# A transformer layer with butterfly networks on one core: loads in a fixed order, one order of work for each sequence, W_up transposed in two halves, the second folded matrix built on GpSimd

## The chip, the core and the metric

The kernel runs on one core of a Trainium2 chip. The metric is the device time of one execution in microseconds. Before the change the median of three runs is 900.11 us (900.03 to 900.91). Engines are called by the profile's names: PE (matrix products), PEld (its weight loads), DVE (VectorE), ACT (ScalarE), POOL (GpSimd), SP (the queue from which most DMAs are issued).

## The reference

Eight sequences of 512 rows and 256 columns go through a feed-forward block, attention and the same feed-forward block again, all in float32:

```python
def ffn(x):                                   # used twice, with the same weights
    h = x @ W_exp + b_exp                     # 256 -> 1024
    h = butterfly(h, up_weights, 1024)        # 10 stages of 2x2 mixes, stride 2**stage
    h = gelu(h + up_bias)
    h = butterfly(h, down_weights, 1024)
    return h @ W_con + b_con + down_bias      # 1024 -> 256

x = x + 0.5 * ffn(layernorm(x))
x = x + attention(layernorm(x))               # 16 heads of 32 (two halves of 16), causal softmax, then @ Wo
x = x + 0.5 * ffn(layernorm(x))
```

A butterfly is linear, so W_exp with the first network is one 256x1024 matrix W_up, and the second network with W_con one 1024x256 matrix W_dn.

## The kernel before

**The start (lines 613 to 632)** builds W_up and W_dn once on the chip. `low_matrices` (L201) multiplies the seven low stages of a network into one 128x128 matrix for each of 8 blocks of rows: six elementwise products at L223 with 32, 64, ..., 1024 elements per partition, on DVE. `low_up` (L244) multiplies the blocks of W_exp by them on PE. `high_stage` (L227) does one of the three high stages: for each of 8 blocks ACT or POOL scales the block itself (L236, L238, into `mine`), and DVE adds the scaled partner block (L241). `finish_up` (L261) transposes the result on PE with 16 transposes (L267) and copies it to `wup_sb` in four copies, two on ACT and two on DVE (L268). Then come the up products of sequence 0 (`up_steps`, L307 on PE, the Gelu at L314 on ACT), three between the stages of the second network; the second network's matrices (DVE, ahead of them), its three high stages, and `low_down` (L270), whose products (L273) make W_dn. `keep_busy(26)` (L255) runs 26 filler products at the very start. Row norms are `ln_stats` (L148: DVE, and POOL for the power at L158) and `ln_apply` (L165); `ffn_bias` (L186) adds half of the two output biases to x on POOL (L189). The order of instructions in this part is that of the program, engine by engine.

**The loads (lines 117 to 135)** are issued from SP and ACT ahead of that part, without `manual_schedule`, so that the framework orders them.

**The main part (lines 634 to 636)** walks through 8 sequences. For each, `sequence` (L573) reads a string of tokens from `ORDER` and issues the work of each token, which fixes the order of every engine's queue. A token is a letter and a number; a digit ahead repeats it, and "+1" or "-1" behind it means that the work belongs to the next or the last sequence. On an entry "None" falls whatever sequence has no string of its own (1 to 4 here).

- f, F: one up product (128 hidden columns: L307, Gelu L314) and half a down product (L325; the sum into x at L334) of the first block; g, G the same of the second block, whose result is stored (L336). F and G fill one PSUM bank with two row tiles, t = 0 and 1, then 2 and 3.
- q, v, w: products for query or key (L350), value (L368), and output (L505).
- u: the scores of one of ten units (L404), then on DVE the mask and the row's minimum (L418), then the exponential on ACT (L431). The scores have one buffer of four banks (`ps_u`).
- t: DVE's transpose of exponentials within 32x32 blocks (L449, L453); m: the sums (L458, L459) and 16 DMAs that move the blocks to other partitions (L471, tile `pt`, one buffer); p: probabilities times values (L484), scaled into `ot` (L491).
- s, a, x with a, 1 or 2 behind: row norm's statistics, its application, and its transposition, which for most sequences is a DMA to memory (L287) and four back (L294). l: load a sequence's x (four buffers).

Products of q, v, f, F, g, G and w all take one of three PSUM buffers (`ps_a`).

Of the kernel before, what the change touches and what calls it, by code (L numbers as in the profile page):

```python
# [36 lines left out]
F32 = mybir.dt.float32  # L37
# [11 lines left out]
def macaron_kernel(  # L49
# [55 lines left out]
    def load_x(b):  # L105
        xt[b] = resid.tile([P, NT, C], F32, name=f"x_{b}", tag="x", bufs=4)
        nc.sync.dma_start(out=xt[b], in_=x[b].rearrange("(t p) c -> p t c", p=P))
# [7 lines left out]
    wdn_sb = const.tile([P, NBLK, C], F32, name="wdn_sb")  # L115

    last = upe_sb.shape[1] - NBLK * P
    nc.sync.dma_start(out=upe_sb[:, :last], in_=up_e[:, :last])
    nc.sync.dma_start(out=upe_sb[:, last:], in_=up_e[:, last:])
    for blocks in (slice(0, NBLK // 2), slice(NBLK // 2, NBLK)):  # L120
        nc.sync.dma_start(out=wexp_sb[:, blocks, :], in_=wexp_t.rearrange("(n p) c -> p n c", p=P)[:, blocks, :])
        if blocks.start == 0:
            load_x(0)
    nc.scalar.dma_start(out=upc_sb, in_=up_c)
    nc.scalar.dma_start(out=bc_sb, in_=b_con.to_broadcast([P, C]))
    nc.scalar.dma_start(out=db_sb, in_=dn_b.to_broadcast([P, C]))
    nc.scalar.dma_start(out=upb_sb, in_=up_b)
    nc.scalar.dma_start(out=dnc_sb, in_=dn_c)
    nc.sync.dma_start(out=dne_sb, in_=dn_e)
    nc.sync.dma_start(out=wcon_sb, in_=wcon.rearrange("(n p) c -> p n c", p=P))  # L130
    load_x(1)
    for w_sb, w in ((wq_sb, wq), (wk_sb, wk), (wv_sb, wv), (wo_sb, wo)):
        nc.sync.dma_start(out=w_sb, in_=w.rearrange("(k p) f -> p k f", p=P))
    for b in range(2, 4):
        load_x(b)


    ident = const.tile([P, P], F32, name="ident")
# [59 lines left out]
    kept = {}  # L198


    def low_matrices(tables, net):  # L201

        at, mat = 0, None
        for step in range(LOW):
            half = 1 << step
            mine = tables[:, at : at + NBLK * 2 * half].rearrange("p (n e) -> p n e", n=NBLK)  # L210
            at += NBLK * 2 * half
            if mat is None:
                mat = mine
                continue
            new = fold_pool.tile([P, NBLK, 2 * half], F32, name=f"mat_{net}_{step}", tag=f"mat_{step % 2}")
            if net == "up":
                dims, old = "p n (a r) -> p n a r", mat.rearrange("p n (o r) -> p n o r", o=1)
                shape = dict(a=2)
            else:
                dims, old = "p n (m b) -> p n m b", mat.rearrange("p n (m o) -> p n m o", o=1)  # L220
                shape = dict(b=2)
            view = new.rearrange(dims, **shape)
            nc.vector.tensor_tensor(view, mine.rearrange(dims, **shape), old.to_broadcast(view.shape), ALU.mult)  # L223
            mat = new
        return mat

# [31 lines left out]
        for _ in range(times):  # L258
            nc.tensor.matmul(idle[:, :P], lhsT=ident, rhs=ident, start=True, stop=True)  # L259

    def finish_up(cur, whole):  # L261
        nc.gpsimd.tensor_tensor(bup_sb, whole[:, :, C], upb_sb, ALU.add)
        for q in range(NBLK // 4):
            for kc in range(KC):
                pt = ps_a.tile([P, 512], F32, name=f"pup_{kc}_{q}", tag="a")
                for i in range(4):
                    nc.tensor.transpose(pt[:, bass.ts(i, P)], cur[4 * q + i][:, bass.ts(kc, P)], ident)  # L267
                (nc.vector.tensor_copy if kc else nc.scalar.copy)(wup_sb[:, kc, bass.ts(q, 512)], pt)  # L268

    def low_down(mats, cur):  # L270
        for blk in range(NBLK):
# [46 lines left out]
    def down_steps(b, what, store):  # L318
        def step(t, half):
            t2, i = divmod(t, 2)  # L320
            if i == 0 and half == 0:
                kept["py", what, b] = ps_a.tile([P, 512], F32, name=f"py_{what}_{b}_{t2}", tag="a")
            g, py = kept["g", what, b], kept["py", what, b].rearrange("p (t c) -> p t c", c=C)
            for fc in range(half * NBLK // 2, (half + 1) * NBLK // 2):
                nc.tensor.matmul(  # L325
                    py[:, i, :],
                    lhsT=g[:, fc, bass.ts(t, P)],
                    rhs=wdn_sb[:, fc, :],
                    start=(fc == 0),
                    stop=(fc == NBLK - 1),  # L330
                )
            if i == 1 and half == 1:
                mine = xt[b][:, 2 * t2 : 2 * t2 + 2, :]
                nc.vector.scalar_tensor_tensor(mine, py, 0.5, mine, ALU.mult, ALU.add)  # L334
                if store:
                    nc.sync.dma_start(  # L336
                        out=out[b, bass.ds(2 * t2 * P, 2 * P), :].rearrange("(t p) c -> p t c", p=P), in_=mine
                    )

        return [partial(step, t, half) for t in range(NT) for half in range(2)]  # L340
# [177 lines left out]
    def run(*steps):  # L518
        for step in steps:
            if isinstance(step, list):  # L520
                run(*step)
            else:
                step()

    def attention_steps(b, pool):
        def moved(g):
# [15 lines left out]


    ORDER = {
        0: """3F+0 x1+1 F+0 2s1+2 sa+0 F+0 x1+1 3F+0 sa+0 2aa+0 2f+1 2xa+0 a1+2 f+1 q+0 a1+2 q+0 f+1 u0 q+0 v u1
              2q+0 t0 x1+2 t1b q+0 u2 t1a v t2a f+1 m0 2f+1 u3 f+1 v t2b u4 F+1 t3 F+1 v x1+2 u5 t4a 2F+1 t4b sa+1
              p0 m1 2F+1 aa+1 t5 2F+1 q+0 sa+1 u6 aa+1 q+0 t6b xa+1 u7 xa+1 t6a t7a p1 m2 u8 2q+1 u9 t8 t7b t9b
              2q+1 t9a 3q+1 p2 q+1 m3""",
        None: """u0 5f+1 u1 f+1 t1a 2f+1 u2 t0 p-3 v u3 t2a 3w-1 t1b m0 s2-1 w-1 v s2-1 u4 v 2F+1 a2-1 s1+2 a2-1 F+1
              t3 F+1 t2b x2-1 s1+2 F+1 v u5 t4a p0 t4b 2F+1 x2-1 m1 F+1 g-1 sa+1 4g-1 aa+1 2g-1 t5 sa+1 aa+1 g-1  # L550
              u6 2G-1 u7 p1 G-1 xa+1 t6a xa+1 q+1 t7a t6b m2 G-1 q+1 u8 t7b a1+2 t8 a1+2 q+1 x1+2 G-1 q+1 G-1 u9
              2G-1 x1+2 t9a t9b q+1 p2 q+1 l+3 m3 2q+1""",
        5: """u0 3f+1 s1+2 u1 f+1 s1+2 f+1 u2 t0 f+1 p-3 t1a t1b u3 2w-1 t2a s2-1 2w-1 m0 2f+1 u4 v s2-1 2a2-1 v
              t2b F+1 t4a t3 3F+1 u5 x2-1 a1+2 2v F+1 x2-1 t4b a1+2 u6 x1+2 p0 F+1 m1 F+1 u7 F+1 sa+1 2g-1 sa+1
              aa+1 2g-1 t7a aa+1 g-1 xa+1 t5 t6a 2g-1 xa+1 u8 t6b p1 m2 g-1 G-1 u9 2G-1 q+1 t8 t9b G-1 t7b q+1
              x1+2 q+1 2G-1 t9a p2 m3""",
        6: """u0 q+0 G-2 u1 G-2 f+1 t1b t1a q+0 u2 f+1 t0 q+0 f+1 t2b u3 t2a p-3 m0 q+0 u4 v l+2 t3 w-1 f+1 u5 w-1
              t4b t4a w-1 s2-1 w-1 2v a2-1 v u6 p0 m1 f+1 q+0 3f+1 t6b t6a t5 s2-1 u7 a2-1 3F+1 x2-1 u8 x2-1 F+1
              t7a p1 m2 u9 sa+1 3F+1 t9b F+1 2g-1 sa+1 2aa+1 t9a g-1 xa+1 g-1 t8 g-1 t7b g-1 p2 g-1 xa+1 g-1 m3
              3q+1""",  # L560
        7: """u0 q+0 u1 G-2 t0 G-2 u2 p-3 w-1 v t1a G-2 t1b t2a m0 u3 G-2 t2b w-1 u4 s2-1 v t4a w-1 t3 w-1 2v s2-1
              t4b p0 m1 2a2-1 2q+0 u5 q+0 u6 q+0 x2-1 G-2 t5 t6b u7 t6a G-2 x2-1 t7a p1 m2 G-2 t7b u8 G-2 2g-1 t8
              g-1 u9 t9b g-1 t9a 2g-1 p2 g-1 m3 g-1 7G-1 p3 2w+0 s2+0 2w+0 s2+0 a2+0 G-1 a2+0 2x2+0 8g+0 8G+0""",
    }
    LNS = {"a": "at", "1": "f1", "2": "f2"}
    queues = {}
# [4 lines left out]
        return queues[key, b].pop(0)  # L571

    def sequence(b, pool):  # L573
        for token in ORDER.get(b, ORDER[None]).split():
            times, rest = (int(token[0]), token[1:]) if token[0].isdigit() else (1, token)
            what, kind, at = rest[0], "", 0
            if what in "sax":
# [33 lines left out]


    with fold, tc.manual_schedule():
        keep_busy(26)
        mats = low_matrices(upe_sb, "up")
        nc.vector.tensor_tensor(bhalf, bc_sb, db_sb, ALU.add)
        nc.vector.tensor_scalar(bhalf, bhalf, 0.5, None, ALU.mult)
        cur = low_up(mats)
        run([partial(ln_stats, 0, "f1", half) for half in range(2)])
        run([partial(ln_apply, 0, "f1", half, nc.gpsimd) for half in range(2)])  # L620
        for i in range(HIGH):
            cur, whole = high_stage(cur, i, upc_sb, "up", C + 1, NBLK)
        run(ln_steps(0, "f1", copy=nc.scalar.copy), partial(ffn_bias, 0, 0), partial(ffn_bias, 0, 1))
        finish_up(cur, whole)
        up = up_steps(0, "f1")
        mats = low_matrices(dne_sb, "dn")
        cur = [wcon_sb[:, blk, :] for blk in range(NBLK)]
        for i in range(HIGH - 1, -1, -1):
            cur, _ = high_stage(cur, i, dnc_sb, "dn", C, NBLK if i == HIGH - 1 else NBLK // 2)
            run([up.pop(0) for _ in range(min(3, len(up)))])  # L630
        low_down(mats, cur)
        run(lns(1, "f1"))

    with tc.tile_pool(name="attn", bufs=1) as attn, tc.manual_schedule():
# [79 lines left out]
```

## Time and profile before

| | us |
|---|---|
| median of three runs | 900.11 |
| the profiled execution | 900.17 |
| its span, first to last instruction | 898.5 |
| PE busy | 871.0 |
| DVE busy | 628.8 |
| ACT busy | 516.0 |
| POOL busy | 87.1 |
| DMA engines, share of the span (queue 1) | 54.9% |

The mean granted clock of PE is 0.989. "Busy" of PE includes the filler products (8.8 us). The span is what the trace covers; the execution's own time is 1.67 us longer. A group's line has the engine, the operation, output and input, the count, then busy time and mean length; the costliest are L325 (233.9 us in 1024 instructions), L307 (229.7 in 512) on PE, and L431 (280.3) and L418 (216.2) on ACT and DVE. A stretch's line has, for each engine, busy time and the number of instructions, in the order PE, PEld, DVE, ACT, POOL, then the granted clock of PE, the share of the DMA engines and GB/s.

### The profile page before, as it was taken

What the parts mean: (1) busy time and instruction counts of PE and PEld (TensorE: products, weight loads), DVE (VectorE), ACT (ScalarE), POOL (GpSimd) and SP (SyncE); (2) the same over time, 40 slices, a digit from 0 to 9 for tenths busy, and PEclk for the clock granted to TensorE, in tenths of its full rate; (3) what the DMA queues carried; (4) which work ended last, traced back from release to release, by engine and by line L of the source; (5) the groups of instructions that cost most, each with busy time, mean ns of one, the idle gap of its engine ahead of it and who ended that gap; (6) DMA issues with size and microseconds to landing.
All of it is one profiled execution on the core that took longest, in us unless ns stands there. A gap on an engine that the chain in (4) does not pass through costs nothing.

```text
span 898.5 us, 13295 instructions
## 1 busy us (share of the span) xinstructions
PE 871.0 (97%) x4348; PEld 502.6 (56%) x4348; DVE 628.8 (70%) x1812; ACT 516.0 (57%) x1356; POOL 87.1 (10%) x103
## 2 busy tenths in 40 slices
PE   6999979999999999999999999999999999999998
PEld 5574633565645655465554656456564573644656
DVE  6966885685838867397675968589868875888230
ACT  4718746944558364763648445695749764756211
POOL 4230000020100201020010201002000010010010
PEclk8899989999999999999999999999999999999999
DMA  9110667366571657546392665816775577477600
GB/s 327 61 47 24 159 186 174 70 177 175 151 201 44 173 136 210 142 117 171 107 249 62 173 170 128 234 53 171 184 191 131 142 199 195 103 177 192 151 12 23
DMA packets 52931, 130.15 MB, mean 145 GB/s; under 512 B 10880, under 2 KB 32640, under 8 KB 52864
## 3 DMA queue, kind: packets, MB, share of 16 engines
q1 hardware_dynamic: 52144, 129.00, 54.9%
q8 instruction: 34, 0.56, 0.3%
q10 hardware_dynamic: 720, 0.32, 0.2%
q14 instruction: 33, 0.27, 0.1%
HBM read 21.80 MB, written 15.20 MB: 41 GB/s over the span
## 4 chain that ended last, share of the span: by engine, by line
PE 88%; DVE 5%; ACT 3%; SPq 2%; DMA 1%; issue 1%; POOL 0%; DVEq 0%; ACTq 0%; POOLq 0%
PE py_f L325 24%; PE ph_f L307 23%; PE pp L350 10%; PE sc L404 9%; PE pa L484 8%; PE pv L368 6%; PE po L505 6%; SPq L471 2%; DVE e L418 2%; ACT e L431 2%; DMA pt<-pr 1%; DVE high_up L241 1%; PE idle L259 1%; ACT L314 1%; DVE pr L449 1%
## 5 line engine op out<-in xcount | busy, mean ns | idle before, releaser
L431 ACT ACTIVATE e<-e,nm 128x128 f32<-128x128 f32 (+3 forms) x512 | 280.3, 549 | 80.1 <-DVE nm L418 79.8
L418 DVE CUSTOM_DVE_ANT_0 e<-sc,mask 128x128 f32<-128x128 f32 (+3 forms) x512 | 216.2, 484 | 141.5 <-PE sc L404 141.4
L325 PE MATMUL py_f<-wdn_sb,g_f 128*128 128x256 f32 x1024 | 233.9, 382 | 0.0
L307 PE MATMUL ph_f<-xnt_f,wup_sb 128*128 128x512 f32 x512 | 229.7, 599 | 2.0 <-ACT g_f L314 2.0
L325 PEld LDWEIGHTS py_f<-wdn_sb,g_f 128*128 128x128 f32 x1024 | 192.0, 190 | 43.7 <-issue 18.1
L449 DVE STREAM_TRANSPOSE pr<-e 128x1536 f32<-128x1536 f32 (+2 forms) x128 | 171.2, 1355 | 19.7 <-ACT e L431 19.7
L307 PEld LDWEIGHTS ph_f<-xnt_f,wup_sb 128*128 128x128 f32 x512 | 95.7, 191 | 118.8 <-issue 101.4
L314 ACT ACTIVATE g_f<-ph_f,bup_sb 128x512 f32<-128x512 f32 x128 | 84.5, 686 | 130.3 <-PE ph_f L307 130.0
L404 PE MATMUL sc<-kt,qt 32*128 32x128 f32 (+3 forms) x1024 | 92.5, 462 | 5.9 <-ACT kt L357 3.3
L431 ACT ACTIVATION_READ_ACCUMULATOR e<-e,nm 128x1 f32 x512 | 95.7, 187 | 0.0
L484 PE MATMUL pa<-pt,v 128*32 128x512 f32 (+3 forms) x1024 | 77.5, 444 | 5.2 <-DMA td_at<-tx_at 2.2
L404 PEld LDWEIGHTS sc<-kt,qt 32*128 32x128 f32 x1024 | 44.4, 183 | 65.3 <-issue 31.8
L158 POOL TENSOR_TENSOR rstd_f<-mv_f,mhalf 128x2 f32<-128x2 f32 x32 | 22.8, 712 | 479.0 <-DVE mv_f L156 479.0
L484 PEld LDWEIGHTS pa<-pt,v 128*32 128x32 f32 x1024 | 31.4, 111 | 59.9 <-issue 54.2
L350 PE MATMUL pp<-xnt_at,wk_sb 128*128 128x512 f32 x128 | 61.3, 601 | 0.0
L350 PE MATMUL pp<-xnt_at,wq_sb 128*128 128x512 f32 x128 | 61.2, 600 | 0.0
L368 PE MATMUL pv<-wv_sb,xnt_at 128*128 128x512 f32 x128 | 60.7, 603 | 0.0
L505 PE MATMUL po<-wo_sb,ot 128*128 128x256 f32 x256 | 58.7, 384 | 0.1
L334 DVE SCALAR_TENSOR_TENSOR x<-py_f,x 128x512 f32<-128x512 f32 x32 | 21.7, 679 | 52.1 <-PE py_f L325 52.1
L505 PEld LDWEIGHTS po<-wo_sb,ot 128*128 128x128 f32 x256 | 47.7, 190 | 13.3 <-ACT e L431 3.3
L189 POOL TENSOR_TENSOR x<-x,bhalf 128x512 f32<-128x512 f32 x32 | 40.8, 1275 | 145.9 <-DVE xn_f L172 111.4
L357 ACT ACTIVATE kt<-pp 128x512 f32<-128x512 f32 x32 | 18.9, 591 | 46.6 <-PE pp L350 46.6
(74 smaller groups left out, 565.1 us busy)
## 6 DMA issues: line engine op xcount, KB each, us to landing
pt<-pr SPq DMA_DIRECT2D x512, 176.0 KB, 4.1
td_f<-tx_f SPq DMA_DIRECT2D x14, 512.0 KB, 4.7
xnt_f<-td_f SPq DMA_DIRECT2D x56, 128.0 KB, 3.1
x<-in_x_dram SPq DMA_DIRECT2D x8, 512.0 KB, 6.1
out_dram<-x SPq DMA_DIRECT2D x16, 256.0 KB, 4.2
td_at<-tx_at SPq DMA_DIRECT2D x7, 512.0 KB, 4.0
xnt_at<-td_at SPq DMA_DIRECT2D x28, 128.0 KB, 3.0
wexp_sb<-in_wexp_t_dram SPq DMA_DIRECT2D x2, 514.0 KB, 7.3
```

Source lines behind the costliest of these rows:

```text
L189: nc.gpsimd.tensor_tensor(x2, x2, bhalf.rearrange("p (o c) -> p o c", o=1).to_broadcast([P, 2, C]), ALU.add)
L307: nc.tensor.matmul(ph[:, :N], lhsT=wup_sb[:, kc, bass.ts(fc, P)], rhs=xnt[:, :, kc, :].rearrange("p i (t r) -> p t i r", r=32), start=(kc ...
L314: nc.scalar.activation(g[:, fc, :], ph[:, :N], AF.Gelu, bias=bup_sb[:, fc : fc + 1])
L325: nc.tensor.matmul(py[:, i, :], lhsT=g[:, fc, bass.ts(t, P)], rhs=wdn_sb[:, fc, :], start=(fc == 0), stop=(fc == NBLK - 1),)
L350: nc.tensor.matmul(pp[:, :N], lhsT=w[:, kc, bass.ts(g, P)], rhs=xnt[:, :, kc, :], start=(kc == 0), stop=(kc == KC - 1),)
L368: nc.tensor.matmul(pp, lhsT=xnt[:, t, kc, :], rhs=wv_sb[:, kc, :], start=(kc == 0), stop=(kc == KC - 1))
L404: nc.tensor.matmul(sc[:, j, at : at + n], lhsT=kept["q", b, gg][r, bass.ts(qb, P)], rhs=kept["k", b, gg][r, :n], start=(i == 0), stop=True ...
L418: nc.vector.tensor_tensor_reduce(out=e[:, j, at : at + n], in0=sc[:, j, at : at + n], in1=mask[:, N - n :], scale=-1.0, scalar=3.0e38, op0 ...
L431: nc.scalar.activation(e[:, j, at : at + n], e[:, j, at : at + n], AF.Exp, scale=-1.0, bias=nm[:, qb, gg, j : j + 1], accum_out=zs[:, gg, ...
L449: nc.vector.transpose(pr[:, :, :, qb : qb + 3 * n - 2 : 3, :].rearrange("p j h k r -> p h k j r"), blocks[:, :, :n])
L484: nc.tensor.matmul(by_row[r, :, kb * 32 :], lhsT=v[:, kb, bass.ds(g * P + j * HD, HD)], rhs=pt[:, :, bass.ds(j * NSLOT + SLOT[kb] + kb, NT ...
L505: nc.tensor.matmul(po[:, i, :], lhsT=ot[:, g, bass.ts(t, P)], rhs=wo_sb[:, g, :], start=(g == 0), stop=(g == NG - 1))
```

## The change

The loads go into a `manual_schedule`, in the order of the program; four small ones move from ACT's queue to SP's, behind the weights of the second network. There are 19 filler products. The second network's matrices are built on POOL, ahead of the high stages of the first. `finish_up` does one half (four blocks) at a time: the first half, the first high stage of the second network, two up products, the second half, and then two up products after each part. The halved bias and its addition to x_0 come after the second network. The last sequence's down product of the second block fills a bank for each row tile, with a sum and a store of its own. Each sequence has its own string of tokens.

```diff
-    nc.sync.dma_start(out=upe_sb[:, :last], in_=up_e[:, :last])
...
+    with tc.manual_schedule():
+        nc.sync.dma_start(out=upe_sb[:, :last], in_=up_e[:, :last])
+        nc.sync.dma_start(out=upe_sb[:, last:], in_=up_e[:, last:])
+        nc.sync.dma_start(out=wexp_sb[:, first, :], in_=wexp_blocks[:, first, :])
+        load_x(0)
+        nc.sync.dma_start(out=wexp_sb[:, second, :], in_=wexp_blocks[:, second, :])
+        nc.scalar.dma_start(out=upc_sb, in_=up_c)
+        nc.sync.dma_start(out=dne_sb, in_=dn_e)
+        nc.sync.dma_start(out=wcon_sb, in_=wcon.rearrange("(n p) c -> p n c", p=P))
+        nc.sync.dma_start(out=dnc_sb, in_=dn_c)
+        nc.sync.dma_start(out=upb_sb, in_=up_b)
+        nc.sync.dma_start(out=bc_sb, in_=b_con.to_broadcast([P, C]))
+        nc.sync.dma_start(out=db_sb, in_=dn_b.to_broadcast([P, C]))
+        load_x(1)
...
-            nc.vector.tensor_tensor(view, mine.rearrange(dims, **shape), old.to_broadcast(view.shape), ALU.mult)
+            engine.tensor_tensor(view, mine.rearrange(dims, **shape), old.to_broadcast(view.shape), ALU.mult)
...
+    def finish_up(cur, whole, q):
+
+        blocks = slice(4 * q, 4 * q + 4)
+        nc.gpsimd.tensor_tensor(bup_sb[:, blocks], whole[:, blocks, C], upb_sb[:, blocks], ALU.add)
+        for kc in range(KC):
+            pt = ps_a.tile([P, 512], F32, name=f"pup_{kc}_{q}", tag="a")
+            for i in range(4):
+                nc.tensor.transpose(pt[:, bass.ts(i, P)], cur[4 * q + i][:, bass.ts(kc, P)], ident)
+            (nc.vector.tensor_copy if kc or q else nc.scalar.copy)(wup_sb[:, kc, bass.ts(q, 512)], pt)
...
+            n = 1 if store and b == B - 1 else 2
+            if i % n == 0 and half == 0:
+                kept["py", what, b] = ps_a.tile([P, 512], F32, name=f"py_{what}_{b}_{t // n}", tag="a")
...
+            if (i + 1) % n == 0 and half == 1:
+                mine = xt[b][:, t + 1 - n : t + 1, :]
+                nc.vector.scalar_tensor_tensor(mine, py[:, i + 1 - n : i + 1, :], 0.5, mine, ALU.mult, ALU.add)
...
     ORDER = {
-        0: """3F+0 x1+1 F+0 2s1+2 sa+0 F+0 x1+1 3F+0 sa+0 2aa+0 2f+1 2xa+0 a1+2 f+1 q+0 a1+2 q+0 f+1 u0 q+0 v u1
-              2q+0 t0 x1+2 t1b q+0 u2 t1a v t2a f+1 m0 2f+1 u3 f+1 v t2b u4 F+1 t3 F+1 v x1+2 u5 t4a 2F+1 t4b sa+1
-              p0 m1 2F+1 aa+1 t5 2F+1 q+0 sa+1 u6 aa+1 q+0 t6b xa+1 u7 xa+1 t6a t7a p1 m2 u8 2q+1 u9 t8 t7b t9b
-              2q+1 t9a 3q+1 p2 q+1 m3""",
-        None: """u0 5f+1 u1 f+1 t1a 2f+1 u2 t0 p-3 v u3 t2a 3w-1 t1b m0 s2-1 w-1 v s2-1 u4 v 2F+1 a2-1 s1+2 a2-1 F+1
...
+        0: """2F+0 s1+2 2F+0 s1+2 F+0 x1+1 2F+0 sa+0 F+0 x1+1 sa+0 2f+1 2aa+0 xa+0 f+1 xa+0 f+1 2q+0 f+1 a1+2 u0
+              q+0 v u1 q+0 v q+0 t0 t1b u2 v t1a t2a f+1 m0 f+1 a1+2 f+1 u3 x1+2 v t2b q+0 u4 3F+1 t3 t4a F+1 u5
+              x1+2 t4b sa+1 F+1 p0 m1 u6 F+1 t5 2F+1 q+0 aa+1 q+0 sa+1 u7 aa+1 f+2 t6a t7a 2f+2 u8 2xa+1 t6b p1 m2
+              t7b 3f+2 q+1 2f+2 q+1 t8 u9 q+1 t9a 2q+1 t9b p2 m3""",
+        1: """u0 q+0 F+1 u1 t0 t1a q+0 2F+1 u2 F+1 q+0 u3 t1b t2a p-3 m0 u4 3w-1 t3 t2b w-1 2v 2s2-1 F+1 2a2-1 F+1
...
+        2: """u0 2q+0 u1 2q+0 t0 l+2 q+0 u2 f+1 q+0 u3 p-3 w-1 t1b t1a w-1 2v f+1 t2a s2-1 s1+2 v m0 t3 u4 a2-1
...
+        7: """2g-2 3q+0 u0 q+0 u1 2G-2 t0 u2 p-3 t1b t1a G-2 t2a m0 w-1 u3 w-1 G-2 u4 v t2b s2-1 2w-1 t4a t3 a2-1
+              2v s2-1 t4b v p0 m1 q+0 a2-1 q+0 u5 q+0 u6 x2-1 G-2 t5 q+0 t6b u7 t6a t7a x2-1 G-2 p1 m2 G-2 u8 G-2
+              l+1 g-1 t8 2g-1 t7b u9 t9a g-1 t9b 2g-1 p2 m3 2g-1 7G-1 p3 2w+0 s2+0 2w+0 s2+0 G-1 2a2+0 2x2+0 8g+0
+              8G+0""",
...
     with fold, tc.manual_schedule():
-        keep_busy(26)
-        mats = low_matrices(upe_sb, "up")
-        nc.vector.tensor_tensor(bhalf, bc_sb, db_sb, ALU.add)
-        nc.vector.tensor_scalar(bhalf, bhalf, 0.5, None, ALU.mult)
+        keep_busy(19)
+        mats = low_matrices(upe_sb, "up", nc.vector)
         cur = low_up(mats)
         run([partial(ln_stats, 0, "f1", half) for half in range(2)])
         run([partial(ln_apply, 0, "f1", half, nc.gpsimd) for half in range(2)])
+        down_mats = low_matrices(dne_sb, "dn", nc.gpsimd)
         for i in range(HIGH):
             cur, whole = high_stage(cur, i, upc_sb, "up", C + 1, NBLK)
-        run(ln_steps(0, "f1", copy=nc.scalar.copy), partial(ffn_bias, 0, 0), partial(ffn_bias, 0, 1))
-        finish_up(cur, whole)
-        up = up_steps(0, "f1")
-        mats = low_matrices(dne_sb, "dn")
...
+        run(ln_steps(0, "f1", copy=nc.scalar.copy))
+        finish_up(cur, whole, 0)
+        up, ups = up_steps(0, "f1"), cur
+        blocks = [wcon_sb[:, blk, :] for blk in range(NBLK)]
+        cur, _ = high_stage(blocks, HIGH - 1, dnc_sb, "dn", C, NBLK)
+        run(up[:2])
+        finish_up(ups, whole, 1)
+        run(up[2:4])
+        up = up[4:]
+        for i in range(HIGH - 2, -1, -1):
+            cur, _ = high_stage(cur, i, dnc_sb, "dn", C, NBLK // 2)
+            run([up.pop(0) for _ in range(2)])
+        nc.vector.tensor_tensor(bhalf, bc_sb, db_sb, ALU.add)
+        nc.vector.tensor_scalar(bhalf, bhalf, 0.5, None, ALU.mult)
+        low_down(down_mats, cur)
+        run(partial(ffn_bias, 0, 0), partial(ffn_bias, 0, 1))
         run(lns(1, "f1"))
```

## The prediction

> **What bounds the kernel now.** I read the busy times first, then busy time by stretches, then the chain of waits of the slow stretches.
>
> ```profile
> span 898.5 us, 13295 instructions
> PE 871.0 (97%) x4348; PEld 502.6 (56%) x4348; DVE 628.8 (70%) x1812; ACT 516.0 (57%) x1356; POOL 87.1 (10%) x103
> ...
> 20.00:30.00 10.00, 7.81 (x27) 5.37 (x27) 8.81 (x17) 6.68 (x16) 2.59 (x3) 0.60 0.69 229
> ...
> 120.00:130.00 10.00, 5.42 (x40) 2.01 (x44) 8.46 (x29) 7.13 (x29) 0.00 (x0) 0.67 0.66 191
> ...
> 140.00:150.00 10.00, 8.62 (x47) 3.54 (x46) 5.77 (x7) 3.85 (x11) 0.00 (x0) 1.00 0.57 128
> ...
> 260.00:270.00 10.00, 9.50 (x36) 3.98 (x34) 1.91 (x11) 6.95 (x12) 0.00 (x0) 1.00 0.66 157
> ```
>
> In the stretches the second number is PE's busy time, the third from the end its granted clock. PE is the bound: from 27.54 us on it hardly stops, one sequence takes 105.6 us of it, and no part of the change removes a multiplication. Only three things can move the end: when PE's dense work starts, the holes in it, and the tail. The holes after 50 us add up to 19.2 us (848.5 less 829.3 busy in the stretches): 6.7 between 110 and 160, 0.5 at each of 260, 360 and 470, 4.9 from 760 to 860, 2.15 at 860 to 870, 3.9 in the tail. In 120 to 130 the clock is down as well.
>
> The chain of waits through the start, and through the hole of sequence 0:
>
> ```profile
> 10.47 1.75 PE low_up L252 x8
> 12.22 0.02 issue
> 12.25 1.58 ACT mine_up L236 x4
> ...
> 23.31 4.23 PE pup L267 x16
> 27.54 13.98 PE ph_f L307 x32
> 41.52 3.64 PE low_dn L273 x16
> ...
> 122.11 3.79 DMA td_at<-tx_at
> 125.90 0.36 issue
> 126.26 4.38 PE pa L484 x32
> ```
>
> Between 13.85 and 26.03 the 24 combining steps of L241 (DVE) set the start; PE then does 16 transposes and goes dense at 27.54. In sequence 0 the product p1 starts at 126.26, when the moved tile lands, and runs 4.38 us where the other products take 2.29: at half clock.
>
> **Loads.** SP's load of x_0 waits now 3.0 us for ScalarE's load of upc. In the change, bc, db, dnc and upb (128+128+24+4 KB) leave the front. The stretches show 306 to 402 GB/s there, so 284 KB are some 0.8 us: x_0, which lands at 10.87 (issued 5.11, median 6.1 us for such loads, DVE starts on it at 10.89), is there at about 10.1. The bounds are 0 (bandwidth is all, order nothing) and 1.75 us (all of DVE's wait for x_0). SP gets four more issues of 0.4 us before x_1, whose first reader runs at 42.66: hidden by 20 us. ScalarE's queue gets shorter, hidden too.
>
> **Filler products, 26 to 19.** By 8.0 us 37 of the 52 filler instructions are counted, so 38 end near 8.2 instead of 10.47. The first product waits then for W_exp's first half (9 us). ScalarE's part starts near 11 instead of 12.25 and no longer holds DVE, whose row norms (2.65 us) run from 10.1 to 12.75. L241 starts at 12.8 instead of 13.85: gain 1.05, bounds 0.3 and 1.8.
>
> **Second matrix on POOL.** Here the change meets DVE. These rows are from the timeline around 20 us (start, duration, engine, line):
>
> ```profile
> 19.66 1.60 DVE L241 SCALAR_TENSOR_TENSOR high_up<-high_up,upc_sb,mine_up 128x257 f32<-128x257 f32 x1
> 19.71 1.27 POOL L189 TENSOR_TENSOR x<-x,bhalf 128x512 f32<-128x512 f32 x1
> 20.94 1.44 POOL L189 TENSOR_TENSOR x<-x,bhalf 128x512 f32<-128x512 f32 x1
> 21.18 1.48 DVE L241 SCALAR_TENSOR_TENSOR high_up<-high_up,upc_sb,mine_up 128x257 f32<-128x257 f32 x1
> ```
>
> A step that elsewhere takes 0.48 us (0.40 from start to start) takes 1.60 and 1.48 beside a two-input POOL operation: each POOL operation costs DVE its own length less about 0.15 us. The trace shows no such build on POOL, so it is priced by L189 (512 elements, 1.27) and L262 (8 elements, 0.20), 2.12 ns an element: six steps of 32, 64, 128, 256, 512 and 1024 take 0.25, 0.32, 0.45, 0.73, 1.27 and 2.37, in all 5.4 us, of which DVE loses 4.4. Bounds: nothing, if POOL's reads and DVE's fall between each other as beside the one-input L172 (17.00 to 19.66: 0.53 a step), and 9.8 us, if the repeated inner element halves POOL's rate. I take 4.4, since L189 is the same operation on the same two engines. The bias additions that cost 2.2 there move behind the second matrix.
>
> So POOL ends the normalised rows at 18.9 (now 19.74). By then DVE has done stage 0 (12.8 to 15.95) and 5.5 of the other 16 steps; 10.5 remain, 4.2 us, and 4.4 are lost: they end at 27.5. The same sum for the kernel before gives 19.66 + 11 x 0.40 + 2.2 = 26.3 against 26.03 measured. The step is 1.5 us late.
>
> The Trainium skill, "SBUF — State Buffer", section "Who interferes with whom", speaks against this edit: a DVE instruction with two SBUF inputs and a GpSimd one that reads SBUF take turns on a shared pair of ports, the later one blocked for the whole of the other. The two rows above agree; L172's 0.53 us a step does not.
>
> DVE no longer builds this matrix (3.2 us at 28.18): worth nothing, since PE runs its 32 products over it from 27.54 to 41.52; without that cover it would be a gain of 3.2. The two late bias additions stand ahead of POOL's row norms for x_1, up to 2.5 us; x_1's transposed rows land at 55.5 now and are read at 58.97, so 3.5 us of slack hide it.
>
> **W_up in halves.** The first up products need the copies of the first half. The one on DVE stands behind all of L241, 25.94 to 26.63 now, so 28.1 in the change, and PE starts the products at 28.2. It then owes what it owed at 27.54 (13.98 us), plus eight transposes that were done before (0.2 each, 1.6), plus the clock. Now the 16 transposes wake the clock: dense from 23.31, full at 27.92, 4.6 us; at 126.26 it took 3.9 until 130.2. In the change PE idles between the eight transposes and 28.2, so the products themselves run at half speed for about 4 us and lose 2.0 (bounds 0 and 3). low_dn starts at 28.2 + 13.98 + 1.6 + 2.0 = 45.8 instead of 41.52: **+4.3 us**. The combining steps of the second matrix come some 3 us earlier on DVE and stay ahead of PE. If POOL costs DVE nothing and the clock is awake, it is 23.8 + 13.98 + 1.6 = 39.4: -2.1. With POOL at half its rate it is +9.7.
>
> The rule on the clock (the Trainium skill, "TensorE: Matmul & The Clock Gate", Part 1) wants about 3.4 us of activity; with it the loss would be 1.7 instead of 2.0. The rows here show 3.9 and 4.6.
>
> **The order.** I counted PE's work between tokens with the rows' durations: f, g, q, v 1.72, F, G 1.73, w 1.78, u 1.08, p 2.29. Tile pt has one buffer, so p(g+1) can't start before move g+1, which starts after p(g): now p0 ends at 107.94 and p1 starts at 126.26, 18.3 us; p1 ends at 130.64 and p2 starts at 146.83, 16.2 us. The work between them counts 12.5 and 14.2 in the old order, 17.0 and 18.3 in the new one, which puts up products of sequence 2 there (some 6% more with switching). The holes 1.05, 1.62, 2.15 and 1.38 go, and the 2.1 us of half clock in p1: 8.3. Of that I leave 0.5 for p1, and 0.7 for "q+0 sa+1 u7", where u7 waits for ScalarE's copy of that q (such a wait is 0.69 at 799.75). **-7.1**; bounds 0 and -8.3.
>
> The four holes of 0.5 (near 157, 260, 360, 470) have one cause: u0, then four f in a row with three PSUM buffers, whose exponentials, table load and Gelu take 5.9 against 5.3 us of PE. I went through all 80 units of the new order: none is followed by too little. **-2.0**; bounds +4 and -2. Sequence 7 keeps its distances of 13.6, 15.9 and 15.6, its "u0 q u1" and "u5 q u6": its 4.9 us stay. DVE's longest backlog against PE by this count falls from 10.5 us (sequence 0, where the hole is) to 9.5 (sequence 2). SP's stores, reads and x_4 to x_7 loads move within their sequences; each load keeps over 10 us to its first reader.
>
> **Last tiles.** The last addition is 128x256 instead of 128x512 (0.69 to 0.41, as L172 and L510 stand to each other) and its store half as long: **-0.5** of the 3.9; bounds 0 and -0.8. G before both applies near 862 shifts DVE work around one 1.27 us POOL addition: 0, plus or minus 0.6.
>
> **Sum.** 4.3 - 7.1 - 2.0 - 0.5 = -5.3 us on the profiled execution's 900.17 (span 898.5 and 1.67 around it), 0.06 over the median of 900.11: **894.8**, its own range 891 to 898.
>
> **Rivals.** *POOL is free and the clock awake*: the start gives -2.1 instead of +4.3, 888.4. For it: L172's 0.53. Against: two rows of 1.5 us. *The hole moves*: p1 still waits for half of it, as m1 comes late behind DVE; with 3.6 us back it is 898.4, and up to 901 with a new wait of two us in one sequence. For it: DVE's 9.5 us backlog in sequence 2. Against: sequence 6 had 9.0 and no hole. *Slower*: POOL builds far slower because each element of the smaller matrix is read twice in the innermost dimension, and holds DVE at the start of everything. From a build of 12.6 us (5.4 + 7.1 of the margin to 901.9) it is slower; at three times the rate's cost, 16.2 us, it would be 905.6. For it: the 0.70 us that POOL takes for 2 elements of a power (L158). Against: DVE built both matrices in equal times, pattern or not.
>
> **Chances.** Forecast 0.57, free POOL 0.15, moved hole 0.13, slow build 0.15. A measurement of this kernel tells about 0.2%, 1.8 us: faster 0.72, same 0.13, slower 0.15. Range 888.5 to 901.5, which leaves out the slow build.
>
> **What will show it.** L241's last up step near 27.5 with single steps of over 1 us; PE's dense work from 28, at half clock for 4 us; low_dn near 46; no hole over 1 us between 110 and 160; no 9.50 in later stretches; sequence 7 as before. I am wrong if low_dn starts before 42 or after 50, or if a new hole of over 2 us stands in sequences 1 to 6.

## The result and the profile after

The changed kernel takes 892.1 us (median of four runs, 891.44 to 892.28), the kernel before 900.43 us on the same chip: ratio 0.9906, 95% interval 0.9889 to 0.9923. The profiled execution took 892.01 us, 8.2 less than the 900.17 of before. The forecast was 894.8 us: the direction is right, and 2.7 us more were won than the sum says. One slow run is left out of all that follows: the first of *start_only* took 2291.93 us, with PE busy for 2277.8 of them, for a cause that stays open.

The page's busy times:

```profile
span 890.2 us, 13293 instructions
PE 865.5 (97%) x4334; PEld 500.9 (56%) x4334; DVE 628.2 (71%) x1809; ACT 519.6 (58%) x1359; POOL 93.2 (10%) x110
```

The stretches that answer to those shown of before:

```profile
20.00:30.00 10.00, 7.06 (x16) 3.49 (x16) 9.39 (x16) 6.20 (x13) 5.87 (x7) 0.58 0.67 225
...
120.00:130.00 10.00, 9.96 (x69) 4.05 (x68) 8.85 (x30) 8.51 (x22) 0.69 (x1) 1.00 0.69 191
...
290.00:300.00 10.00, 9.63 (x80) 6.25 (x79) 7.31 (x18) 2.93 (x8) 0.00 (x0) 1.00 0.27 80
```

PE is still the bound. In 120 to 130 it is busy for 9.96 us at full clock, where it was 5.42 at 0.67: the hole of sequence 0 is gone. From 20 to 30 PE is less busy than before (7.06 against 7.81), and POOL is busy for 5.87 us. The stretch 290 to 300 has a small new gap of 0.37 us.

The chain of waits through the start:

```profile
9.10 1.76 PE low_up L254 x8
...
10.88 1.58 ACT mine_up L238 x4
...
19.18 4.87 DVE high_up L243 x4
...
24.10 1.33 PE pup L270 x5
25.43 5.03 PE ph_f L310 x8
30.45 1.06 PE pup L270 x8
31.51 10.49 PE ph_f L310 x24
42.00 3.64 PE low_dn L276 x16
```

Four combining steps of L243 (L241 before) now take 4.87 us, because POOL is at work beside them. The up products begin at 25.43 and take 5.03 us for eight instructions, half clock at first; then come the second half's transposes, 1.06 us, and the other 24 instructions. The second matrix's product starts at 42.00, 0.5 us later than before (41.52).

PE's own timeline, with the places where it still waits (the wait and its releaser stand in brackets):

```profile
127.80 2.36 PE L489 MATMUL pa<-pt,v 128*32 128x512 f32 x32
...
170.99 1.15 PE L409 MATMUL sc<-kt,qt 32*128 32x384 f32 x16 [0.36 <-DVE nm L423]
...
481.48 5.42 PE L310 MATMUL ph_f<-xnt_f,wup_sb 128*128 128x512 f32 x12 [0.71 <-ACT v L376]
```

The product p1 of sequence 0 has no wait and runs 2.36 us, at full clock. The 0.36 us at 170.99 comes back at seven more places. It is always the same: a unit's scores (L409) wait until DVE has read the last unit's (L423).

### The profile page after: what moved, and what is told of

It reads as the page before. It is cut to its first block, busy times and chain, and to the rows that moved or that the text cites. A ratio compares the mean times of both kernels' runs of the same rounds, so it can differ in the third digit from the quotient of the medians.

```text
span 890.2 us, 13293 instructions
## 1 busy us (share of the span) xinstructions
PE 865.5 (97%) x4334; PEld 500.9 (56%) x4334; DVE 628.2 (71%) x1809; ACT 519.6 (58%) x1359; POOL 93.2 (10%) x110
## 4 chain that ended last, share of the span: by engine, by line
PE 82%; DVE 9%; ACT 3%; DMA 2%; SPq 2%; issue 1%; POOL 0%; DVEq 0%; ACTq 0%; POOLq 0%
PE py_f L330 23%; PE ph_f L310 22%; PE pp L355 12%; PE sc L409 9%; PE pa L489 6%; PE pv L373 5%; PE po L510 5%; DVE e L423 4%; SPq L476 2%; ACT e L436 2%; DVE high_up L243 1%; DVE pr L454 1%; PE idle L261 1%; DMA td_f<-tx_f 1%; DMA pt<-pr 1%
## 5 line engine op out<-in xcount | busy, mean ns | idle before, releaser
L423 DVE CUSTOM_DVE_ANT_0 e<-sc,mask 128x128 f32<-128x128 f32 (+3 forms) x512 | 216.3, 485 | 117.2 <-PE sc L409 117.0
L310 PE MATMUL ph_f<-xnt_f,wup_sb 128*128 128x512 f32 x512 | 232.7, 603 | 1.1 <-ACT v L376 0.7
L330 PE MATMUL py_f<-wdn_sb,g_f 128*128 128x256 f32 x1024 | 232.7, 382 | 0.0
L409 PE MATMUL sc<-kt,qt 32*128 32x128 f32 (+3 forms) x1024 | 92.2, 461 | 6.2 <-DVE nm L423 4.4
L489 PE MATMUL pa<-pt,v 128*32 128x512 f32 (+3 forms) x1024 | 75.5, 435 | 2.3 <-DMA pt<-pr 0.9
L409 PEld LDWEIGHTS sc<-kt,qt 32*128 32x128 f32 x1024 | 44.4, 183 | 57.2 <-issue 23.8
L339 DVE SCALAR_TENSOR_TENSOR x<-py_f,x 128x512 f32<-128x512 f32 (+1 forms) x34 | 22.2, 652 | 56.7 <-PE py_f L330 56.7
L510 PE MATMUL po<-wo_sb,ot 128*128 128x256 f32 x256 | 59.4, 384 | 0.0
L373 PE MATMUL pv<-wv_sb,xnt_at 128*128 128x512 f32 x128 | 59.1, 597 | 0.0
```

What stands on the lines that cost most here:

```text
L310: nc.tensor.matmul(ph[:, :N], lhsT=wup_sb[:, kc, bass.ts(fc, P)], rhs=xnt[:, :, kc, :].rearrange("p i (t r) -> p t i r", r=32), start=(kc ...
L330: nc.tensor.matmul(py[:, i, :], lhsT=g[:, fc, bass.ts(t, P)], rhs=wdn_sb[:, fc, :], start=(fc == 0), stop=(fc == NBLK - 1),)
L373: nc.tensor.matmul(pp, lhsT=xnt[:, t, kc, :], rhs=wv_sb[:, kc, :], start=(kc == 0), stop=(kc == KC - 1))
L409: nc.tensor.matmul(sc[:, j, at : at + n], lhsT=kept["q", b, gg][r, bass.ts(qb, P)], rhs=kept["k", b, gg][r, :n], start=(i == 0), stop=True ...
L423: nc.vector.tensor_tensor_reduce(out=e[:, j, at : at + n], in0=sc[:, j, at : at + n], in1=mask[:, N - n :], scale=-1.0, scalar=3.0e38, op0 ...
L489: nc.tensor.matmul(by_row[r, :, kb * 32 :], lhsT=v[:, kb, bass.ds(g * P + j * HD, HD)], rhs=pt[:, :, bass.ds(j * NSLOT + SLOT[kb] + kb, NT ...
```

## The experiments

All ratios are against the kernel before on the same chip; its medians there were 900.47, 900.1 and 899.6 us.

### The order and the start, each alone

The kernel *order_only* has the start, loads and last tiles of before and the new strings of tokens; *start_only* has the reverse, all of the change but these strings. Of *order_only* the diff shows the first line of one string:

```diff
-        None: """u0 5f+1 u1 f+1 t1a 2f+1 u2 t0 p-3 v u3 t2a 3w-1 t1b m0 s2-1 w-1 v s2-1 u4 v 2F+1 a2-1 s1+2 a2-1 F+1
...
+        1: """u0 q+0 F+1 u1 t0 t1a q+0 2F+1 u2 F+1 q+0 u3 t1b t2a p-3 m0 u4 3w-1 t3 t2b w-1 2v 2s2-1 F+1 2a2-1 F+1
```

> The kernel before with the new orders alone (its own loads, start and last tiles). Theory: nearly all of the 8.3 us lies in the order of the sequences, and the new start gives nothing back (low_dn starts at 42.0 us in the changed kernel, 41.5 before). Then this takes 891.5 to 892.8 us (the changed kernel's 892.1 less 0.5 of start plus 0.5 of tail), with no hole over 1 us between 110 and 160 us. Rival: the earlier loads and the row norms of x_1 in the new start carry part of the gain in sequence 0; then this is 895 or more.

> The changed kernel with the old orders. Theory: the start is worth between -0.5 and +1 us, the last tile -0.5, so 900 to 901 us, with the holes at 120 to 126 and 146 us back at their old size (4.8 and 1.4 us idle). Rival (the start carries part of the gain): 897 or less.

Measured: 892.17 us, ratio 0.9915 (0.989 to 0.994), for the order alone; 899.55 us (nine runs), ratio 0.9992 (0.998 to 1.0003), for the start alone. The order's 0.85% and the start's 0.08% add up to nearly the whole 0.94%, but the four runs of *order_only* lie in two pairs, 890.17 and 890.33, 894.01 and 894.39 us, so that the order's share is known to 0.25% only, some 2 us. Its profile is that of the run of 890.33. So the time comes from the order, the start's gains and losses cancel within 2 us, and the rival that gave the start several us is out.

The start alone was run once more for a profile.

> The changed kernel's start, loads and last tiles with the orders of before, to be looked at in its profile. Theory (the start's gain and loss cancel, and the orders alone fill the hole): the product of the second matrix starts between 41.5 and 42.5 us, holes of 1.0 to 2.2 us stand again at 120 to 127 and at 146, p1 of sequence 0 runs 4 us at half clock, and the four places of 0.5 us are back. Rival (the start shifts the work and fills part of the hole): fewer than 5 us idle between 110 and 160.

Measured: 899.47 us. PE's timeline of it in sequences 0 and 1, and after that two steps of its chain of waits:

```profile
120.56 0.71 PE L409 MATMUL sc<-kt,qt 32*128 32x256 f32 x8 [1.05 <-DVE nm L423]
122.89 0.71 PE L409 MATMUL sc<-kt,qt 32*128 32x256 f32 x8 [1.62 <-ACT kt L362]
124.93 3.64 PE L489 MATMUL pa<-pt,v 128*32 128x512 f32 x32 [1.33 <-DMA pt<-pr]
130.88 1.95 PE L355 MATMUL pp<-xnt_at,wq_sb 128*128 128x512 f32 x4 [1.23 <-DMA xnt_at<-td_at]
145.34 2.36 PE L489 MATMUL pa<-pt,v 128*32 128x512 f32 x32 [0.72 <-PE pp L355]
156.53 3.70 PE L310 MATMUL ph_f<-xnt_f,wup_sb 128*128 128x512 f32 x8 [0.50 <-ACT g_f L317]
...
261.98 3.70 PE L310 MATMUL ph_f<-xnt_f,wup_sb 128*128 128x512 f32 x8 [0.50 <-ACT g_f L317]
```

```profile
22.62 2.34 DVE high_up L243
...
41.26 3.64 PE low_dn L276 x16
```

With the old order the hole is there (6.45 us in six pieces, against 6.7 before), p1 is slow again (3.64 us), and so are the places of 0.5 us. None of the places of 0.36 us stands in it between 160 and 700. The second matrix's product starts at 41.26, a little before the expected 41.5. The single DVE step of 2.34 us is the lock by itself, DVE held up by one operation of POOL: elsewhere a step takes 0.48, and 2.37 was the price of POOL's last operation of 1024 elements.

### Sequence 0 without its cover

> The changed kernel, where in sequence 0 the three up products of sequence 2 ahead of p1 come behind it. The work between p0 and p1 falls from 17.0 to 11.8 us by the rows' durations. Theory: the move's chain (p0, sums, 16 DMAs, landing) takes about 18 us whatever PE does, so 5 us or more of holes come back between p0 and p1, some of it before u8, and the clock may drop; the time is 896 to 900. Rival: the gain of sequence 0 came from the units' and copies' places and not from the cover; then under 2 us of holes.

```diff
-              x1+2 t4b sa+1 F+1 p0 m1 u6 F+1 t5 2F+1 q+0 aa+1 q+0 sa+1 u7 aa+1 f+2 t6a t7a 2f+2 u8 2xa+1 t6b p1 m2
-              t7b 3f+2 q+1 2f+2 q+1 t8 u9 q+1 t9a 2q+1 t9b p2 m3""",
+              x1+2 t4b sa+1 F+1 p0 m1 u6 F+1 t5 2F+1 q+0 aa+1 q+0 sa+1 u7 aa+1 t6a t7a u8 2xa+1 t6b p1 m2
+              t7b 6f+2 q+1 2f+2 q+1 t8 u9 q+1 t9a 2q+1 t9b p2 m3""",
```

Measured: 899.26 us (one run), 7.2 more than the changed kernel. Its PE timeline:

```profile
123.89 1.44 PE L409 MATMUL sc<-kt,qt 32*128 32x512 f32 x8 [2.97 <-DVE nm L423]
...
127.01 4.50 PE L489 MATMUL pa<-pt,v 128*32 128x512 f32 x32 [1.68 <-DMA pt<-pr]
```

Three up products of sequence 2, moved from before p1 to behind it, bring back 4.65 us of waiting, a little less than the 5 expected, and the half clock in p1 (4.50 us). Of the waiting 2.97 us are those of unit u8, which waits for DVE to read the last scores, and 1.68 those of p1 for its moved tile; with p1's own 2.1 us they make 6.8 of the 7.2. So the cover that these products give is what removed the hole.

### The second matrix on DVE

> The changed kernel with the second network's matrices built on DVE, after the second half of W_up, where DVE is idle for 4.05 us. Theory: POOL's six two-input operations hold DVE during the steps of L243; without them the steps end near 22.2 us instead of 25.6 (10.5 steps at 0.40 us from 17.8 on), no step is over 0.75 us, low_dn starts near 38.5 instead of 42.0, and the time is 888.6. Rival: the steps wait for ScalarE's scaled blocks or the loads; then they still end at 25 or later and the time is 891.5 to 892.5. Bound between them: ScalarE's 16 scalings take 0.41 each, so the steps can't be faster than that.

```diff
-        down_mats = low_matrices(dne_sb, "dn", nc.gpsimd)
         for i in range(HIGH):
             cur, whole = high_stage(cur, i, upc_sb, "up", C + 1, NBLK)
...
         finish_up(ups, whole, 1)
+        down_mats = low_matrices(dne_sb, "dn", nc.vector)
```

Measured: 888.0 us, ratio 0.9862 (0.9847 to 0.9877), 4.1 us less than the changed kernel. The same rows of both, first the changed kernel, then *build_dve* (start, duration):

```profile
15.64 9.99 DVE L243 SCALAR_TENSOR_TENSOR high_up<-high_up,upc_sb,mine_up 128x257 f32<-128x257 f32 x16
...
17.81 0.54 POOL L225 TENSOR_TENSOR mat_dn<-dne_sb 128x32 f32<-128x32 f32 x1
18.43 5.33 POOL L225 TENSOR_TENSOR mat_dn<-dne_sb,mat_dn 128x64 f32<-128x64 f32 x5
```

```profile
14.76 6.76 DVE L243 SCALAR_TENSOR_TENSOR high_up<-high_up,upc_sb,mine_up 128x257 f32<-128x257 f32 x16
...
28.71 3.00 DVE L225 TENSOR_TENSOR mat_dn<-dne_sb,mat_dn 128x64 f32<-128x64 f32 x5
```

The 16 steps take 6.76 us instead of 9.99 when POOL's build is gone: 3.2 us are what the lock costs. The build itself takes 5.9 us on POOL and 3.2 on DVE, where it lies behind the up products and holds nobody up. The second matrix's product starts at 38.34 instead of 42.00. Four other profiles with the changed kernel's start have it at 41.26 (*start_only2*), 41.39 (*hold*), 41.48 (*uncover_p1*) and 41.52 (*mend*), so the start gains 2.9 to 3.7 us.

### Filler products over the clock's gap

> The changed kernel with eight filler products on PE ahead of the first half's transposes, where PE waits for DVE. Theory: the first up products run at half clock (8 instructions in 5.03 us instead of 3.44) because PE idles before them; with the fillers the clock is awake by about 26 and low_dn comes 1.0 to 1.6 us earlier, near 40.7; time 890.6 to 891.1. Rival: eight fillers in 3.5 us are too few or end too early, and nothing changes.

```diff
         run(ln_steps(0, "f1", copy=nc.scalar.copy))
+        keep_busy(8)
         finish_up(cur, whole, 0)
```

Measured: 890.32 us, ratio 0.9894 (0.988 to 0.9908). A stretch of the changed kernel, then the same of *wake* (the third number from the end is the granted clock):

```profile
24.00:26.00 2.00, 1.90 (x6) 1.43 (x7) 2.00 (x6) 1.39 (x4) 0.58 (x2) 0.50 1.00 319
26.00:28.00 2.00, 2.00 (x4) 0.68 (x3) 2.00 (x6) 2.00 (x7) 0.00 (x0) 0.50 0.24 76
```

```profile
24.00:26.00 2.00, 1.20 (x3) 0.38 (x3) 2.00 (x6) 2.00 (x6) 0.34 (x2) 1.00 0.94 301
```

In the chain of waits of *wake* the second matrix's product:

```profile
40.39 3.65 PE low_dn L276 x16
```

With fillers the clock is full when the products begin, and the second matrix starts 1.6 us earlier than in the changed kernel's profile, 0.9 to 1.1 earlier than in the four others with that start. The clock's loss itself is read from the changed kernel's own rows: 5.03 + 10.49 us for products that take 13.98 before, 1.5 us. The times alone don't settle it, since the interval of *wake* overlaps that of the changed kernel (0.9889 to 0.9923).

### The units with only a p between them

> The changed kernel with eight places of its orders mended: where a unit follows a product p that follows a unit (u, p, u), one product token from behind is put between p and the second unit. Theory: the eight holes of 0.36 us (PE waits for DVE's reading of the scores, 2.65 us against 2.29 of p) are the new orders' own price, so they go and the time is 892.1 - 2.9 = 889.2. Rival: the work put there is missed where it was taken from, or DVE stays behind; then 891 or more.

```diff
-        1: """u0 q+0 F+1 u1 t0 t1a q+0 2F+1 u2 F+1 q+0 u3 t1b t2a p-3 m0 u4 3w-1 t3 t2b w-1 2v 2s2-1 F+1 2a2-1 F+1
+        1: """u0 q+0 F+1 u1 t0 t1a q+0 2F+1 u2 F+1 q+0 u3 t1b t2a p-3 m0 v u4 3w-1 t3 t2b w-1 v 2s2-1 F+1 2a2-1 F+1
...
-              t6a g-1 s1+2 G-1 u7 a1+2 G-1 a1+2 G-1 xa+1 x1+2 2G-1 t7a u8 p1 x1+2 m2 u9 t9b G-1 q+1 2G-1 t8 2f+2
+              t6a g-1 s1+2 G-1 u7 a1+2 G-1 a1+2 G-1 xa+1 x1+2 2G-1 t7a u8 p1 x1+2 m2 G-1 u9 t9b q+1 2G-1 t8 2f+2
...
```

Eight such places are mended. Measured: 889.53 us, ratio 0.9881 (0.9867 to 0.9895), 2.6 us less than the changed kernel (2.3 by the ratios, whose intervals just overlap). All eight waits are gone; what is left of PE's waits between 160 and 740 is one line:

```profile
479.94 5.42 PE L310 MATMUL ph_f<-xnt_f,wup_sb 128*128 128x512 f32 x12 [0.75 <-ACT v L376]
```

### Holding the clock near the end

> The changed kernel with 11 filler products in the gap before the last up products, where PE waits 1.48 and 0.94 us for the last row norm (7 before the first transposes, 4 between the first two and the last two of one half). Theory: the last up products take 15.70 us in the changed kernel, 14.00 with the new orders alone and 14.68 before, for the same instructions, because the clock falls or not after this gap; with the fillers they take 13.7 to 14.1, the time falls by 1 to 2 us in the median, to 890.1 to 891.1, and the runs spread less than 892.28 - 891.44. Rival: the clock falls because of something else, and the fillers only delay the transposes: 892 or more.

```diff
+            if (b, what, kc, t) == (B - 1, "f2", 0, 1):
+                keep_busy(4)
...
-              l+1 g-1 t8 2g-1 t7b u9 t9a g-1 t9b 2g-1 p2 m3 2g-1 7G-1 p3 2w+0 s2+0 2w+0 s2+0 G-1 2a2+0 2x2+0 8g+0
+              l+1 g-1 t8 2g-1 t7b u9 t9a g-1 t9b 2g-1 p2 m3 2g-1 7G-1 p3 2w+0 s2+0 2w+0 s2+0 G-1 7k 2a2+0 2x2+0 8g+0
...
+                elif what == "k":
+                    keep_busy(1)
```

Measured: 891.76 us, ratio 0.9906 (0.9893 to 0.992): the ratio is that of the changed kernel, and the time lies between the theory's and the rival's. The four runs lie 0.88 us apart, those of the changed kernel 0.84, so they agree no more closely. Its PE timeline before the last up products:

```profile
851.97 3.66 PE L263 MATMUL idle<-ident 128*128 128x128 f32 x14
...
855.69 1.16 PE L263 MATMUL idle<-ident 128*128 128x128 f32 x8
...
857.85 14.00 PE L312 MATMUL ph_f<-xnt_f,wup_sb 128*128 128x512 f32 x32 [0.35 <-DVE xnt_f L200]
```

The clock held: the 32 instructions take 14.00 us instead of 15.70. But seven fillers take 3.66 us in a gap of 1.48 and delay the transposes behind them: from the end of the down products to the first of these up products it is 5.7 us instead of 4.4. So 1.3 of the 1.7 us are given back. The fillers were too many.

### Everything together

> The second matrix on DVE (888.0 alone), the eight mended places and the fillers of the last gap together. If the three don't touch each other: 888.0 - 2.9 - 1 to 2 = 883.1 to 884.1, low_dn near 38.3. Rival: with the start 3.7 us earlier or the orders mended another wait stands behind (the moves, p1 in sequence 0), and it is 886 or more.

The kernel *best* has the edits of *build_dve*, *mend* and *hold*. Measured: 886.15 us, ratio 0.9841 (0.9828 to 0.9855), 2 us more than expected. That is the rival's time but not its cause: the profile shows no new wait between 42 and 740 us. What it shows is the 5.7 us of the long fillers again, and down products that take 233.9 us, as in *mend*, where the changed kernel has 232.7. The kernel *best2* differs in the number of fillers alone:

```diff
-              l+1 g-1 t8 2g-1 t7b u9 t9a g-1 t9b 2g-1 p2 m3 2g-1 7G-1 p3 2w+0 s2+0 2w+0 s2+0 G-1 7k 2a2+0 2x2+0 8g+0
+              l+1 g-1 t8 2g-1 t7b u9 t9a g-1 t9b 2g-1 p2 m3 2g-1 7G-1 p3 2w+0 s2+0 2w+0 s2+0 G-1 3k 2a2+0 2x2+0 8g+0
...
-                keep_busy(4)
+                keep_busy(2)
```

> The build on DVE, the mended units and shorter fillers near the end: 3 filler products instead of 7 after the last stored tile's half and 2 instead of 4 between the last transposes. A filler instruction there took 0.26 us, so 3 products (6 instructions) take 1.6 us and 2 take 0.6 to 1.0, as long as the gaps of 1.48 and 0.94 us. Theory (the long fillers gave back what they saved): the transposes end some 1.3 us earlier than with the long ones, the last 32 up-product instructions still take 14.0 us, and the time is 884.6 to 885.2 instead of 886.15. Rival (the short fillers no longer hold the clock): the 32 instructions take 15 to 16.5 us and the time is 885.8 to 887. Rival (something else in the mended order gave the 2 us back): 886.2 with the transposes early and the clock up.

Measured: 884.39 us (883.67 to 885.3), ratio 0.9827 (0.9814 to 0.984): 7.7 us less than the change (7.1 by the ratios), 15.2 less than the kernel before. Its PE timeline:

```profile
847.14 1.48 PE L263 MATMUL idle<-ident 128*128 128x128 f32 x6
...
849.18 0.61 PE L263 MATMUL idle<-ident 128*128 128x128 f32 x4
...
851.73 14.00 PE L312 MATMUL ph_f<-xnt_f,wup_sb 128*128 128x512 f32 x32 [0.35 <-DVE xnt_f L200]
```

The down products end at 847.30 and the up products begin 4.4 us later, as in the changed kernel (852.82 and 857.24). So the shorter fillers cost nothing and the clock still holds. By the ratios *best2* is 1.3 us faster than *best*, as much as 4.4 is less than 5.7, and most of the missing 2 us; the two intervals overlap, so the timeline carries this more than the times do.

## Why the prediction was right, and where its sum was off

| term | forecast, us | measured, us | from |
|---|---|---|---|
| start | +4.3 | +0.5 | second matrix's product 41.52 to 42.00 |
| order, 110 to 160 | -7.6 | -8.7 | PE's idle time in 110 to 160: 6.73 to 0.08; p1 4.38 to 2.36 |
| holes in sequences 1 to 6 | -1.5 | +2.1 | PE's idle time in 160 to 740: 1.49 to 3.63 |
| sequence 7 | 0 | +0.5 | PE's idle time 4.93 to 5.46 |
| before and in the last up products | 0 | +1.6 | wait 2.15 to 2.77; 32 instructions 14.75 to 15.70 |
| tail | -0.5 | -0.5 | from PE's end to the span's: 3.90 to 3.45 |
| not in the sum | | -3.7 | the remainder to -8.2 |

Of the forecast's four places of 0.5 us one, near 157, is counted in the second row and three in the third. That the sum is only 2.9 us off is in part luck: the start was forecast 3.8 us too dear; the small holes, sequence 7 and the last up products together 5.7 us too cheap; the order's gain 1.1 too small; and 3.7 us were won where the sum has no term.

**The order** was right in place, cause and sign. The hole went because PE has work between the products of one buffer, and it comes back when that work is taken away (*uncover_p1*). The 0.5 left for p1 and the 0.7 for "u7 behind q" didn't appear.

**The start** is the term that was mis-sized. Its mechanism is right: POOL locks DVE, and without POOL's build the start gains 2.9 to 3.7 us (*build_dve*). Three of its numbers were too high.

First, L243 ends at 25.63, not at 27.5. x_0 is read from 8.95 us on, 1.9 us earlier than before and not 0.8, which is beyond the bound of 1.75. DVE's row norms end at 11.6, but the filler products end at 9.10 instead of 8.2, so DVE waits 0.90 us for ScalarE's part and the combining steps begin at 12.49. POOL's rows end at 17.84 instead of 18.9, and the lock takes 3.2 us of DVE instead of 4.4.

Secondly, the sentence "PE starts the products at 28.2" makes the products wait for DVE's copy of the first half. That copy runs from 25.55 to 26.23, and they start before it has ended, at 25.43, since the first instructions need only the half that ACT copies. The rule itself isn't wrong: in *mend*, with the same start but earlier transposes, the third instruction does wait for the copy:

```profile
25.64 4.54 PE L310 MATMUL ph_f<-xnt_f,wup_sb 128*128 128x512 f32 x6 [2.31 <-DVE wup_sb L271]
```

Thirdly, the transposes cost 1.06 instead of 1.6 and the clock 1.54 instead of 2.0. With 25.43 in place of 28.2 and these two, the forecast's own sum gives 25.43 + 13.98 + 1.06 + 1.54 = 42.01; measured 42.00. These numbers come from the same rows, so this shows that no term is missing, and tests nothing else.

On the lock, the Trainium skill ("SBUF — State Buffer", "Who interferes with whom") says that the later one of two such instructions waits for the whole of the other. The changed kernel's rows of POOL's operation of 1024 elements agree:

```profile
21.57 2.18 POOL L225 TENSOR_TENSOR mat_dn<-dne_sb,mat_dn 128x1024 f32<-128x1024 f32 x1
21.70 2.34 DVE L243 SCALAR_TENSOR_TENSOR high_up<-high_up,upc_sb,mine_up 128x257 f32<-128x257 f32 x1
```

DVE's step takes POOL's 2.18 us and 0.16 more. A step alone would have taken 0.48, so it loses 1.86, POOL's length less 0.3, where the forecast took off 0.15. POOL's smallest operations cost DVE next to nothing: beside those of 0.38 and 0.49 us its steps take 0.52 and 0.49. That is how all six cost DVE 3.2 us of POOL's 5.9.

**The small holes.** The four of 0.5 us went as forecast. But the step "I went through all 80 units of the new order: none is followed by too little" failed: at eight places only a p lies between two units, 2.29 us of PE, and the scores' one buffer is free only 2.65 us after the last unit, when DVE has read it. The 0.36 us left over, eight times, is 2.9 us. *mend*, without them, is 2.6 us faster; its start came 0.5 us earlier (41.52 for the second matrix's product), and its down products took 1.2 us more.

**What the sum left out.** Some 3.7 us of the gain stand in none of the rows above it. In the groups by line, the same 128 value products took 60.7 us before and 59.1 after, the 1024 down products 233.9 and 232.7; the 256 output products rose from 58.7 to 59.4. *order_only* has 59.1 and 232.7 too, so it is the order. Four instructions of a product behind a u or p (tiles of 32 rows) count 1.91 us and 1.72 elsewhere; the new order has 80 such changes and the old one 90, which makes 1.9 us by this count. *mend*, which breaks up runs of products, has 88 changes and is back at 59.4 and 233.9. The eight transposes ahead of the last up products took 2.2 us before and 1.7 after, another 0.5. The other 1.3 us remain open.

**The rivals.** The second matrix on POOL is not free: DVE's 16 steps lose 3.2 us by it, although the whole start comes to only +0.5. The hole has not moved; no wait of over 1 us is left between 110 and 160. POOL's build takes 5.9 us, near the priced 5.4 and far from 12.6. Of the signs named in the forecast, the single steps of over 1 us, the half clock of the first products, the hole and, nearly, sequence 7 (5.46 us of waiting against 4.93) came true; the end of L243 near 27.5, dense work from 28 and low_dn near 46 did not. The forecast called itself wrong if low_dn starts before 42. In the changed kernel's profile it starts at 42.00, but in the four others with the same start at 41.26 to 41.52: by its own sign the start's step was wrong.

## What to carry to other kernels

Where one engine is busy for 97% of the time, list its waits one by one and count for each the work that another order could put under it: here one such place was worth 8.7 us. The same count, made for every pair of neighbours that share a buffer, would have found the eight small waits. Work moved to an idle engine is only free if the two engines don't lock each other out: here the build on an idle POOL cost 4 us more than on DVE, which had room for it a little later. Filler products belong into gaps that put the clock down, cut to the length of the gap.

## What the runs showed of the hardware

The clock near the end is not set by the gaps alone. These are the changed kernel and *order_only*, with the same waits before the same 32 instructions:

```profile
854.30 0.89 PE L197 MATMUL pxt_f<-ident,xn_f 128*128 128x128 f32 x3 [1.48 <-DVE xn_f L174]
...
857.24 15.70 PE L310 MATMUL ph_f<-xnt_f,wup_sb 128*128 128x512 f32 x32 [0.35 <-DVE xnt_f L198]
```

```profile
853.72 0.89 PE L195 MATMUL pxt_f<-ident,xn_f 128*128 128x128 f32 x3 [1.49 <-DVE xn_f L172]
...
856.66 14.00 PE L307 MATMUL ph_f<-xnt_f,wup_sb 128*128 128x512 f32 x32 [0.35 <-DVE xnt_f L196]
```

Two stretches of each, at the last of these waits (again the changed kernel, then *order_only*; the third number from the end is the granted clock):

```profile
854.34:857.75 3.41, 2.12 (x9) 1.17 (x10) 2.99 (x5) 0.00 (x0) 2.63 (x2) 1.00 0.23 77
857.75:861.16 3.41, 3.41 (x5) 1.28 (x4) 0.03 (x1) 0.52 (x1) 0.00 (x0) 0.50 0.00 0
```

```profile
854.11:857.52 3.41, 2.12 (x9) 1.15 (x9) 2.67 (x4) 0.00 (x0) 2.49 (x2) 1.00 0.23 77
857.52:860.93 3.41, 3.41 (x9) 1.52 (x8) 0.00 (x0) 1.22 (x2) 0.00 (x0) 1.00 0.00 0
```

In the first the granted clock falls to 0.50 at 857.75 and is full again 3.41 us later; in the second it stays at 1.00. In *build_dve* the same work takes 16.53 us. The Trainium skill ("TensorE: Matmul & The Clock Gate", Part 1) says that the gate watches a window that runs freely. The clock's records here fit a window: in all eleven profiles in which the clock changes, every stretch from one change to the next is a whole multiple of 3.41 us. But PE's busy time in the window doesn't tell the two cases apart, since it is 2.12 us ahead of the fall and 2.12 us where no fall follows. What does stays open. Of the profiles without fillers in this gap seven show the fall and *order_only* does not; of the three with them (*hold*, *best*, *best2*) none does. So up to 2.5 us of this kernel's time depend on whether the clock falls there. Each of these numbers is from a single profiled execution.
